# Layer 0 of a two-layer cross-attention kernel: TensorE in four 64x64 tiles, with two PSUM banks for each product

## The chip, the cores and the metric

The kernel runs on one core of a Trainium2 chip. The time is the device time of one execution in microseconds (us): 2881.49 us, the median of three runs (2879.67 to 2883.18).

The core has a matrix engine (TensorE, PE in the profile), which multiplies a stationary operand, loaded beforehand (PEld), with a moving one and writes to PSUM; three engines for the rest (VectorE is DVE, ScalarE is ACT, GpSimd is POOL); and DMA queues, most of them issued by SyncE (SP). Each engine runs its own list of instructions in the written order, and semaphores make one wait for another.

TensorE's array of 128x128 cells can be split into tiles. "128*64" in a profile row means 128 rows (contraction) by 64 columns (outputs) for one tile, so that two such tiles fill the array. Each tile takes its own matmuls.

## The reference

Four batches, two layers of cross-attention, all in 32-bit floats. `x` is 4 x 1024 x 512, the context 4 x 1024 x 384, and there are 16 heads in each layer.

```
layer 0 (heads of 64):
  h = layernorm(x) * gamma + beta
  Q = h Wq;  K = context Wk;  V = context Wv
  A = softmax(Q K^T) / 8
  x = x + (A V) Wo + bo
layer 1 (heads of 32):
  xn = x / rms(x) * norm_w
  q = xn wq;  k, v = split(context wkv)
  q, k = rotate(q), rotate(k), each scaled to length 1
  x = x + (softmax(q k^T * sqrt(32)) v) wout
```

## The kernel before

Everything is one program, written out by Python. For each batch, layer 0 comes first and then layer 1. Layer 0 takes the 16 heads as eight pairs (`p`), as two heads fill 128 partitions. Within a pair there are eight steps (`i`), one for each 128 queries; the class `Attention0` (line 355) writes one step:

- `scores` (line 363): four matmuls of 64 rows by 128 columns, 512 keys each, into two PSUM tiles of two banks, one for each head. The two heads run in two row tiles.
- For each head the negated maximum on DVE (line 393), the exponential on ACT with its sum (394), on DVE the transposition of the step before (402) and the reciprocal (398), on POOL the scaling (399).
- After every second step `regroup` (408) sends the transposed weights to other partitions, in 16 DMAs on SP's queue.
- `product` (421): once two blocks of two steps are queued, the odd step multiplies the older one with V: 8 x 2 matmuls of 128 rows by 64 columns, 256 queries each, into one PSUM bank, which ACT copies out (line 138).
- Then `Units.fill` (71) puts other TensorE work into the rest of the step.

This other work is a queue of small units, each with a cost in us: the projections of the next but one pair (`pair_units`, line 311: K in 6 units, Q in 8, V in 8), the output sums of finished pairs (`add_units`, line 287; a DVE addition for each 128 rows, line 296), and in the last two pairs the first projections of layer 1. Each goes through the helper `matmul` (line 161), which splits the outputs into two column tiles in layer 0 and four in layer 1. The driver (from line 757) counts what is still to be done in the batch, spreads it evenly over the steps that are left, and takes off 3.5 us where a step has a product; `fill` pops units until the sum that is owed is used up. So TensorE's list within a step is: scores, perhaps a product, then units.

PSUM has eight banks here. Four belong to the two score tiles. The other four are handed out in turn by `bank` (line 128), to products, projections, transpositions and sums.

The order on ACT follows the same writing order: both exponentials of a step, the copy of the product, and then the copies of the units of that step.

Layer 1 (`Attention1`, line 556) has 64 steps a batch, with scores in four row tiles (32*128) and everything else in four column tiles (128*32). During its second half, the first projections of the next batch's layer 0 are made.

Of the kernel before, what the change touches and what calls it, by code (L numbers as in the profile page):

```python
# [38 lines left out]
P = 128  # L39
S = 1024  # L40
# [15 lines left out]

class Units:


    def __init__(self):  # L60
        self.todo = deque()
        self.owed = 0.0
        self.done = 0

    def add(self, units):
        self.todo.extend(units)

    def total(self):
        return sum(c for c, _ in self.todo)

    def fill(self, us):
        self.owed += us
        while self.todo and self.owed > 0:
            self.owed -= self.one()
        if not self.todo:
            self.owed = min(self.owed, 0.0)

    def one(self):
        c, f = self.todo.popleft()
        f()  # L80
        self.done += 1
        return c

    def end(self):

        return self.done + len(self.todo)

    def until(self, end):
        while self.done < end:
            self.owed -= self.one()  # L90
# [20 lines left out]
def xattn_kernel(ctx: ExitStack, tc: tile.TileContext, a: dict, out: bass.AP):  # L111
# [14 lines left out]
    which = {"n": 0, "from": 0, "cols": 2, "kept": None}  # L126

    def bank(name):

        while True:  # L130
            which["n"] = which["n"] + 1 if which["n"] < 3 else which["from"]
            if which["n"] != which["kept"]:
                break
            which["kept"] = None
        return ps_f.tile([P, 512], F32, tag=f"f{which['n']}", name=name)
# [31 lines left out]

    def rsqrt(o, v):

        nc.gpsimd.tensor_tensor(o, v, nhalf[:, : v.shape[1]], ALU.pow)  # L170


    def context_units(b, ct):
# [11 lines left out]
        def turn_over(h, k):  # L185
            if k == 0:
                if h == 0:
                    both = sb.tile([P, NC_, S], F32, tag="ctxT", bufs=1, name=f"cT_{b}")
                    ct.extend([both[:, :, :512], both[:, :, 512:]])
            pp = bank(f"ptc_{b}_{h}_{k}")  # L190
            for t in range(4):
                nc.tensor.transpose(pp[:, t * P : (t + 1) * P], raws[4 * h + t][:, k * P : (k + 1) * P], ident)
            evac(ct[h][:, k, :], pp)

# [8 lines left out]
    def norm_units(b, layer, hT, rows):  # L203
# [39 lines left out]
        def turn_over(h, k):  # L243
            if k == 0:
                hT.append(sb.tile([P, NQ, 512], F32, tag="hT", bufs=2, name=f"hT{layer}_{b}_{h}"))
            pp = bank(f"pth{layer}_{b}_{h}_{k}")
            for t in range(4):
                nc.tensor.transpose(pp[:, t * P : (t + 1) * P], got[h][t][:, k * P : (k + 1) * P], ident)
            if layer == 0:
                nc.scalar.activation(  # L250
                    hT[h][:, k, :], pp, AF.Identity, bias=cols[:, 1, k : k + 1], scale=cols[:, 0, k : k + 1]
                )
            else:
                nc.scalar.activation(hT[h][:, k, :], pp, AF.Copy, scale=cols[:, 2, k : k + 1])

# [31 lines left out]
    def add_units(xt, lhs, w, name, cs, then=None):  # L287
# [3 lines left out]
        def one(t, i, pp=[None]):  # L291
            if i == 0:
                pp[0] = bank(f"{name}_{t}")
            matmul(pp[0], lhs(cs[i])[:, t * P : (t + 1) * P], w(cs[i]), i == 0, i == n - 1)
            if i == n - 1:
                nc.vector.tensor_add(xt[t], xt[t], pp[0])  # L296
                if then is not None:
                    then(t)

        return [[(0.86, lambda t=t, i=i: one(t, i)) for i in range(n)] for t in range(NT)]  # L300
# [10 lines left out]
    def pair_units(b, p, w, hT, ct, res):  # L311

        n = f"{b}_{p}"

        def project(what, src, w0, nk, h, k, st={}):
            if what == "kT" and h == 0 and k == 0:
                qk = sb.tile([P, 2, S], F32, tag="qk", bufs=3, name=f"qk0_{n}")
                res["kT"], res["qT"] = qk[:, 0], qk[:, 1]
            if k == 0:
                st["pp"] = bank(f"p{what}0_{n}_{h}")  # L320
            matmul(st["pp"], w()[:, w0 + k, :], src[h][:, k, :], k == 0, k == nk - 1)
            if k < nk - 1:
                return
            if what == "qT":
                evac(res[what][:, h * 512 : (h + 1) * 512], st["pp"])
            else:
                quarters = res[what].rearrange("p (g c i) -> p c g i", g=4, i=32)
                evac(quarters[:, 4 * h : 4 * h + 4], st["pp"].rearrange("p (c g i) -> p c g i", g=4, i=32))

        def values(h, t, st={}):  # L330
            if h == 0 and t == 0:
                res["v"] = sb.tile([P, NT, P], F32, tag="v", bufs=3, name=f"v0_{n}")
            if t == 0:
                st["pp"] = bank(f"pv0_{n}_{h}")
            for k in range(NC_):
                matmul(
                    st["pp"][:, t * P : (t + 1) * P],
# [5 lines left out]
            if t == 3:  # L343
                evac(res["v"][:, 4 * h : 4 * h + 4, :].rearrange("p t f -> p (t f)"), st["pp"])

        return {
# [8 lines left out]
    class Attention0:  # L355
# [7 lines left out]
        def scores(self, p, i, pr):  # L363
            n = f"{self.b}_{p}_{i}"
            sc = [score(f"s0_{n}_{j}") for j in range(2)]
            for kb in range(2):
                for j in range(2):
                    nc.tensor.matmul(  # L368
                        sc[j][:, kb * 512 : (kb + 1) * 512],
                        pr["qT"][r[j], i * P : (i + 1) * P],  # L370
                        pr["kT"][r[j], kb * 512 : (kb + 1) * 512],
                        start=True,
                        stop=True,
                    )
            return sc

        def step(self, p, i, pr, us):
            n = f"{self.b}_{p}_{i}"
            sc = self.scores(p, i, pr)
            m = sb.tile([P, 2], F32, tag="m", bufs=3, name=f"m_{n}")  # L380
# [25 lines left out]
            self.u.fill(us)  # L406
# [14 lines left out]
        def product(self):  # L421
# [4 lines left out]
            av = bank(f"av_{self.b}_{p}_{q}")  # L426
            for k in range(NT):
                for j in range(2):
                    nc.tensor.matmul(  # L429
                        av[r[j], :W].rearrange("p (t a i) -> p t a i", t=BQ, a=4),  # L430
                        pr["v"][:, k, r[j]],
                        eT[:, j, :, :, k * 32 : (k + 1) * 32],
                        start=k == 0,
                        stop=k == NT - 1,
                    )
            evac(pr["vals"][:, q * W : (q + 1) * W], av[:, :W])
# [16 lines left out]
    def rotated_chains(dst, src, nk, w, name, tmp):  # L453
# [10 lines left out]
        def project(t0, i, k):  # L464
            if i == 0 and k == 0:
                tiles[t0] = [bank(f"{name}_p{t0}")]
                if which["from"] == 0:
                    which["kept"] = which["n"]
            pp = tiles[t0][0]
# [3 lines left out]
            if i == TH - 1 and k == nk - 1:  # L473
                rotate(t0, pp)

# [19 lines left out]
        def turn_over(t0):  # L495
            t1 = tiles.pop(t0)
            pt = bank(f"{name}_t{t0}")
# [7 lines left out]
            nc.scalar.copy(dst()[:, :, t0 * P : (t0 + TH) * P], pt.rearrange("p (g t) -> p g t", g=2))  # L505

# [30 lines left out]
    def value_chains(v, wv, ct, name):  # L537
        def one(t0, i, k, st={}):
# [4 lines left out]
            matmul(st["pp"][:, i * FH : (i + 1) * FH], lhsT, wv[:, k, :], k == 0, k == NC_ - 1)  # L543
            if i == TH - 1 and k == NC_ - 1:
                pv = st["pp"].rearrange("p (t g d) -> p g t d", t=TH, g=2)
                for g in range(2):
                    nc.scalar.copy(v[g][:, t0 : t0 + TH, :], pv[:, g])

# [141 lines left out]
    def prepare_units(b):  # L690
# [7 lines left out]
        def project(p):  # L698
# [5 lines left out]
            return begin | pair_units(b, p, lambda: w[p], st["hT"], st["ct"], st["pairs"][p])  # L704
# [5 lines left out]
        def order(other):  # L710

            pairs = [project(p) for p in range(2)]
# [24 lines left out]
            ), pairs[1]["v"]  # L737
# [3 lines left out]
    work = Units()  # L741
    st, order = prepare_units(0)
# [14 lines left out]
    for b in range(B):  # L757
# [7 lines left out]
        for p in range(NPAIR):  # L765
# [10 lines left out]
            elif p % 2 == 0:  # L776
# [6 lines left out]
                    (p - 2, p - 1),  # L783
                )
# [29 lines left out]
            n = 7 * (p == 0)  # L814
# [58 lines left out]
        for half in range(2):  # L873
            n = 0
            if half == 0:
# [11 lines left out]
                base = work.done  # L887
# [41 lines left out]
        which["from"], which["cols"] = 0, 2  # L929
        if b == B - 1:  # L930
            tail = flat(adds[1][6:])
        else:
            outs = add_units(
                xt, lambda n, o=o: o[n], lambda n, w=wo1[1]: w[:, n % 2, :], f"po1_{b}_1", (2, 3), store
# [40 lines left out]
```

## Time and profile before

| what | us |
|---|---|
| median of three runs | 2881.49 |
| span of the profiled execution | 2885.9 |
| PE busy | 2827.9 |
| DVE busy | 2248.4 |
| ACT busy | 1430.1 |
| layer 0 scores (line 368), 2048 records | 519.1 |
| layer 0 products (line 429), 4096 records | 472.8 |
| layer 0 maxima on DVE (line 393), 512 | 602.9 |
| layer 0 transpositions on DVE (line 402), 512 | 619.9 |

The profile is that of one execution; its span, 2885.9 us, is its own time from the first to the last instruction, and it is 0.15% above the median of the runs. A 32-bit matmul shows as two records of weight load and two of matmul. The records' durations overlap, so the sum of a group is more than the time it takes; the distance between the starts of two groups tells what the first one cost. In four stretches, one for each batch, the eight pairs of layer 0 take about 444, 429, 430 and 430 us.

### The profile page before, as it was taken

What the parts mean: (1) busy time and instruction counts of PE and PEld (TensorE: products, weight loads), DVE (VectorE), ACT (ScalarE), POOL (GpSimd) and SP (SyncE); (2) the same over time, 40 slices, a digit from 0 to 9 for tenths busy, and PEclk for the clock granted to TensorE, in tenths of its full rate; (3) what the DMA queues carried; (4) which work ended last, traced back from release to release, by engine and by line L of the source; (5) the groups of instructions that cost most, each with busy time, mean ns of one, the idle gap of its engine ahead of it and who ended that gap; (6) DMA issues with size and microseconds to landing.
All of it is one profiled execution on the core that took longest, in us unless ns stands there. A gap on an engine that the chain in (4) does not pass through costs nothing.

```text
span 2885.9 us, 65749 instructions
## 1 busy us (share of the span) xinstructions
PE 2827.9 (98%) x26888; PEld 1420.5 (49%) x26888; DVE 2248.4 (78%) x3008; ACT 1430.1 (50%) x2276; POOL 947.8 (33%) x776
## 2 busy tenths in 40 slices
PE   8999999999999999999999999999999999999998
PEld 4444445555444445555544445455554444445543
DVE  5677786898777778589877777959987777785987
ACT  4443443666444444466643444446664444444664
POOL 2343344320134335342023433534202333353410
PEclk9999999999999999999999999999999999999999
DMA  5887776010298777501039887740105887773000
GB/s 138 183 188 176 174 170 150 22 37 25 73 207 189 180 173 174 128 22 36 26 93 205 195 184 165 178 103 22 37 26 121 203 196 184 163 173 83 2 2 31
DMA packets 177549, 348.81 MB, mean 121 GB/s; under 512 B 37600, under 2 KB 93152, under 8 KB 177248
## 3 DMA queue, kind: packets, MB, share of 16 engines
q1 hardware_dynamic: 175920, 343.96, 50.9%
q8 instruction: 212, 3.47, 0.5%
q14 instruction: 89, 0.73, 0.1%
q10 hardware_dynamic: 1328, 0.66, 0.1%
HBM read 67.64 MB, written 8.39 MB: 26 GB/s over the span
## 4 chain that ended last, share of the span: by engine, by line
PE 87%; DVE 3%; SPq 3%; DMA 2%; ACT 2%; issue 1%; POOL 1%; ACTq 0%; DVEq 0%
PE s L368 16%; PE av L429 14%; PE po L166 11%; PE s L586 9%; PE av L635 8%; PE pv L166 7%; PE pqT L166 7%; PE pkT L166 5%; PE q_p L166 4%; PE k_p L166 3%; SPq L413 2%; DMA eT<-e 1%; ACT e L596 1%; PE av L659 1%; DVE m L393 1%
## 5 line engine op out<-in xcount | busy, mean ns | idle before, releaser
L393 DVE TENSOR_REDUCE m<-s 128x1 f32<-128x1024 f32 x512 | 602.9, 1219 | 381.5 <-PE s L368 380.9
L596 ACT ACTIVATE e<-s 128x1024 f32<-128x1024 f32 x512 | 496.5, 1022 | 295.3 <-PE s L586 288.9
L399 POOL TENSOR_SCALAR raw<-raw,li 128x1024 f32<-128x1024 f32 x256 | 286.1, 1118 | 734.1 <-DVE li L398 725.6
L368 PE MATMUL s<-qk 64*128 64x512 f32 x2048 | 519.1, 616 | 3.0 <-ACT e L394 2.2
L394 ACT ACTIVATE e<-s,m 128x1024 f32<-128x1024 f32 x256 | 282.8, 1109 | 465.2 <-DVE m L393 224.3
L394 ACT ACTIVATE raw<-s,m 128x1024 f32<-128x1024 f32 x256 | 285.1, 1114 | 458.7 <-DVE m L393 458.7
L429 PE MATMUL av<-eT,v 128*64 128x256 f32 x4096 | 472.8, 384 | 12.2 <-DMA eT<-e 9.1
L399 POOL TENSOR_SCALAR e<-e,li 128x1024 f32<-128x1024 f32 x256 | 286.1, 1118 | 472.6 <-DVE li L398 240.3
L429 PEld LDWEIGHTS av<-eT,v 128*64 128x64 f32 x4096 | 288.2, 137 | 232.1 <-issue 94.8
L605 DVE TENSOR_TENSOR both<-e 128x512 f32<-128x512 f32 x512 | 342.8, 702 | 64.3 <-ACT e L596 62.2
L368 PEld LDWEIGHTS s<-qk 64*128 64x128 f32 x2048 | 184.8, 186 | 285.2 <-issue 168.8
L586 PE MATMUL s<-q,k 32*128 32x256 f32 x4096 | 308.0, 402 | 5.3 <-ACT q L505 2.7
L402 DVE STREAM_TRANSPOSE e<-raw 128x1024 f32<-128x1024 f32 x256 | 309.9, 1228 | 1.7 <-DMA eT<-e 1.7
L402 DVE STREAM_TRANSPOSE e<-e 128x1024 f32<-128x1024 f32 x256 | 310.0, 1229 | 0.2
L586 PEld LDWEIGHTS s<-q,k 32*128 32x128 f32 x4096 | 193.9, 185 | 142.5 <-ACT e L596 66.4
L166 PE MATMUL pqT<-hT,w 128*64 128x512 f32 (+1 forms) x1216 | 241.9, 597 | 2.5 <-ACT hT L250 2.5
L166 PE MATMUL po<-wo,vals 128*64 128x512 f32 x1024 | 234.6, 596 | 0.0
L166 PEld LDWEIGHTS pv<-w,cT 128*64 128x64 f32 (+1 forms) x3360 | 170.4, 132 | 41.8 <-issue 34.1
L296 DVE TENSOR_TENSOR x<-x,po 128x512 f32<-128x512 f32 x200 | 131.7, 678 | 70.4 <-PE po L166 69.7
L166 PE MATMUL pv<-w,cT 128*64 128x128 f32 (+1 forms) x3360 | 184.3, 274 | 0.9 <-ACT hT L250 0.7
L166 PE MATMUL pkT<-cT,w 128*64 128x512 f32 (+1 forms) x912 | 182.0, 597 | 0.0
L607 DVE TENSOR_TENSOR both<-both 128x1024 f32<-128x1024 f32 x128 | 159.7, 1248 | 4.4
(87 smaller groups left out, 2801.3 us busy)
## 6 DMA issues: line engine op xcount, KB each, us to landing
eT<-e SPq DMA_DIRECT2D x2048, 128.0 KB, 2.4
xr<-in_x_dram SPq DMA_DIRECT2D x32, 256.0 KB, 4.0
wo<-in_Wo_dram SPq DMA_DIRECT2D x16, 512.0 KB, 3.9
x<-in_x_dram SPq DMA_DIRECT2D x32, 256.0 KB, 5.0
out_dram<-x SPq DMA_DIRECT2D x32, 256.0 KB, 2.7
w<-in_Wq_dram SPq DMA_DIRECT2D x31, 256.0 KB, 3.3
c<-in_ctx_dram SPq DMA_DIRECT2D x32, 192.0 KB, 3.9
wkv<-in_wkv_dram SPq DMA_DIRECT2D x16, 384.0 KB, 3.3
```

What stands on the lines that cost most here:

```text
L166: nc.tensor.matmul(o[rr], lhsT[:, rr], rhs, start=start, stop=stop)
L368: nc.tensor.matmul(sc[j][:, kb * 512 : (kb + 1) * 512], pr["qT"][r[j], i * P : (i + 1) * P], pr["kT"][r[j], kb * 512 : (kb + 1) * 512], st ...
L393: nc.vector.tensor_reduce(m[:, j : j + 1], sc[j], AX.X, ALU.max, negate=True)
L394: nc.scalar.activation(e[j], sc[j].rearrange("p (g s) -> p g s", g=4), AF.Exp, bias=m[:, j : j + 1], accum_out=l[:, j : j + 1])
L399: nc.gpsimd.tensor_scalar(e[j], e[j], li[:, j : j + 1], HD0**-0.5, ALU.mult, ALU.mult)
L402: self.turn = [lambda j=j: nc.vector.transpose(self.e[:, :, i % BQ * 2 + j, :], e[j]) for j in range(2)]
L429: nc.tensor.matmul(av[r[j], :W].rearrange("p (t a i) -> p t a i", t=BQ, a=4), pr["v"][:, k, r[j]], eT[:, j, :, :, k * 32 : (k + 1) * 32], ...
L586: nc.tensor.matmul(sc[j // 2][:, j % 2, c, :], kT[rr, g, k * P : (k + 1) * P], qT[rr, g, qb * WQ : (qb + 1) * WQ], start=True, stop=True,)
L596: nc.scalar.activation(e, sc[u], AF.Exp, scale=float(np.sqrt(np.float32(HD1))))
L605: nc.vector.tensor_add(into[:, 2 * u : 2 * u + 2, :], es[u][:, :, 0, :], es[u][:, :, 1, :])
L607: nc.vector.tensor_add(acc, acc, into)
L635: nc.tensor.matmul(self.av[rr, 0, :], v[g][:, 2 * kk + c, rr], es[j // 2][:, j % 2, c, :], start=first and c == 0, stop=end and c == 1,)
```

## The change

Everything that layer 0 does on TensorE within its steps is put into tiles of 64 rows by 64 columns, of which four fill the array.

- Scores: each matmul is split into two of 64 queries.
- Products: the contraction over 128 keys is split into two halves, in two row tiles, each of which writes its own bank. ACT copies the first bank and DVE adds the second.
- Projections of layer 0 and output sums: two results are made together, in a pair of banks (0, 1) or (2, 3). In a first turn row tile 0 works for the first result and row tile 1 for the second; in the second turn they change over. Row tiles must not write one bank at once, so between the turns there is a barrier: a copy of one element on ACT (`turned`) waits for the first turn's last matmul, and the second turn's first matmul waits for this copy.
- The planner: such a double result is a `Group` with two turns. The second turn counts as ready when 1.5 us of other TensorE work has passed since the first (`RIPE`). A second group may be begun when the first isn't ready and a pair of banks is free. In even steps (`spare`) no group is begun if what is owed doesn't reach to end the open one, and groups are ended until at most one pair of banks is held, since the next step's product needs the other.
- Banks: the one (or the pair) that has been free the longest is taken, instead of one after the other.

Layer 1 keeps its shapes, and so do the first pair's projections, the last output sum of layer 0 and the transpositions. The diff, cut to its core:

```diff
+class Group:
+    def __init__(self, turns):
+        self.turns = [deque(t) for t in turns]
+        self.since = 0.0
+    def left(self):
+        return sum(c for t in self.turns for c, _ in t)
...
 class Units:
+    RIPE = 1.5
...
-    def fill(self, us):
+    def passed(self, us):
+        for _, g in self.open:
+            g.since += us
+    def fill(self, us, spare=False):
         self.owed += us
-        while self.todo and self.owed > 0:
+        while (self.todo or self.open) and self.owed > 0:
+            if spare and self.open and self.starts_next() and self.owed < self.open[0][1].left():
+                break
             self.owed -= self.one()
+        while spare and self.pairs_held() > 1:
+            self.owed -= self.one()
...
+    def ready(self):
+        return [g for _, g in self.open if g.turns[0] or g.since >= self.RIPE]
+    def starts_next(self):
+        return not self.ready() and self.todo and isinstance(self.todo[0], Group) and self.pairs_held() < 2
+    def pick(self):
+        ready = self.ready()
+        if ready:
+            return ready[0]
+        if self.starts_next():
+            g = self.todo.popleft()
+            self.open.append((self.begun, g))
+            self.begun += 1
+            return g
+        if self.todo and not isinstance(self.todo[0], Group):
+            return None
+        return self.open[0][1]
     def one(self):
-        c, f = self.todo.popleft()
+        g = self.pick()
...
+        turn = next(t for t in g.turns if t)
+        c, f = turn.popleft()
         f()
-        self.done += 1
+        self.passed(c)
+        if not g.turns[0] and turn is g.turns[0]:
+            g.since = 0.0
...
-    which = {"n": 0, "from": 0, "cols": 2, "kept": None}
+    which = {"from": 0, "cols": 2, "clock": 0}
+    freed, held = [0, 1, 2, 3], set()
...
     def bank(name):
-        while True:
-            which["n"] = which["n"] + 1 if which["n"] < 3 else which["from"]
-            if which["n"] != which["kept"]:
-                break
-            which["kept"] = None
-        return ps_f.tile([P, 512], F32, tag=f"f{which['n']}", name=name)
+        n = min((n for n in range(which["from"], 4) if n not in held), key=lambda n: freed[n])
+        return take([n], [name])[0]
+    def two_banks(name):
+        free = [p for p in ((0, 1), (2, 3)) if not held & set(p)]
+        p = min(free, key=lambda p: max(freed[n] for n in p))
+        return take(p, [f"{name}_a", f"{name}_b"])
+    def free(n, later=0):
+        which["clock"] += 1
+        held.discard(n)
+        freed[n] = which["clock"] + later
...
+    sixty = [slice(j * 64, (j + 1) * 64) for j in range(2)]
+    turned = const.tile([1, 1], F32, name="turned")
+    def behind(inst, other):
+        tc.add_manual_dep(inst.ins, other.ins.name, SYNC, reason="row tiles change banks")
+    def quarters(st, os, lhsTs, rhss, turn, start, stop, last):
+        for i in range(2):
+            u = i ^ turn
+            for j in range(2):
+                mm = nc.tensor.matmul(
+                    os[u][sixty[j]], lhsTs[u][sixty[i], sixty[j]], rhss[u][sixty[i]], start=start, stop=stop
+                )
+                if turn == 1 and st["turned"] is not None:
+                    behind(mm, st["turned"])
+                    st["turned"] = None
+        if turn == 0 and last:
+            st["turned"] = nc.scalar.copy(turned, ident[:1, :1])
+            behind(st["turned"], mm)
...
+        def project_both(what, src, w0, nk, k, turn, st):
+            first, last = k == turn == 0, k == nk - 1 and turn == 1
...
+            if first:
+                st["pp"] = two_banks(f"p{what}0_{n}")
+            quarters(
...
+            if last:
+                for h in range(2):
+                    placed(what, h, st["pp"][h])
...
+                "k": group(0.86, NC_, lambda k, turn, st: project_both("kT", ct, NQ, NC_, k, turn, st)),
+                "q": group(0.86, NQ, lambda k, turn, st: project_both("qT", hT, 0, NQ, k, turn, st)),
+                "v": group(0.66, 4, values_both),
...
 def scores(self, p, i, pr):
...
                 for j in range(2):
-                    nc.tensor.matmul(
-                        sc[j][:, kb * 512 : (kb + 1) * 512],
-                        pr["qT"][r[j], i * P : (i + 1) * P],
...
+                    for q in range(2):
+                        q0 = i * P + q * 64
+                        nc.tensor.matmul(
+                            sc[j][sixty[q], kb * 512 : (kb + 1) * 512],
+                            pr["qT"][r[j], q0 : q0 + 64],
...
             sc = self.scores(p, i, pr)
+            self.u.passed(1.71)
...
                 self.product()
-            self.u.fill(us)
+                self.u.passed(3.41)
+            self.u.fill(us, spare=i % BQ == 0)
...
-            av = bank(f"av_{self.b}_{p}_{q}")
+            av = two_banks(f"av_{self.b}_{p}_{q}")
             for k in range(NT):
-                for j in range(2):
...
+                for n, (_, pp) in enumerate(av):
+                    for j in range(2):
+                        nc.tensor.matmul(
+                            pp[r[j], :W].rearrange("p (t a i) -> p t a i", t=BQ, a=4),
+                            pr["v"][sixty[n], k, r[j]],
+                            eT[sixty[n], j, :, :, k * 32 : (k + 1) * 32],
...
-            evac(pr["vals"][:, q * W : (q + 1) * W], av[:, :W])
+            vals = pr["vals"][:, q * W : (q + 1) * W]
+            evac(vals, av[0][1][:, :W])
+            free(av[0][0])
+            nc.vector.tensor_add(vals, vals, av[1][1][:, :W])
+            free(av[1][0])
...
+    work.pairs_held = lambda: sum(bool(held & set(p)) for p in ((0, 1), (2, 3)))
...
-            n = 7 * (p == 0)
+            n = 2 * (p == 0)
```

## The prediction

> **What bounds the kernel now.** I read the page first, then TensorE's own order in time, then all engines over two steps of layer 0, then the busy times of one batch's layer 0.
>
> ```profile
> span 2885.9 us, 65749 instructions
> PE 2827.9 (98%) x26888; PEld 1420.5 (49%) x26888; DVE 2248.4 (78%) x3008; ACT 1430.1 (50%) x2276; POOL 947.8 (33%) x776
> ...
> PE 87%; DVE 3%; SPq 3%; DMA 2%; ACT 2%; issue 1%; POOL 1%; ACTq 0%; DVEq 0%
> ```
>
> TensorE (PE) is the bound: 98% busy, 87% of the chain that ended last. Whether that is useful work is seen in its order in time (start, duration, engine, line, tiles, shape, count):
>
> ```profile
> 203.37 1.99 PE L368 MATMUL s<-qk 64*128 64x512 f32 x8
> 205.28 3.67 PE L429 MATMUL av<-eT,v 128*64 128x256 f32 x32
> 208.79 1.48 PE L166 MATMUL pv<-w,cT 128*64 128x128 f32 x24
> 210.20 1.99 PE L368 MATMUL s<-qk 64*128 64x512 f32 x8
> 212.11 2.84 PE L166 MATMUL pv<-w,cT 128*64 128x128 f32 x48
> 214.78 1.89 PE L166 MATMUL po<-wo,vals 128*64 128x512 f32 x8
> 216.60 1.99 PE L368 MATMUL s<-qk 64*128 64x512 f32 x8
> ```
>
> Two tiles run at once, and two records of 512 columns take 0.428 us (from the distances inside the weight loads of one projection: 901.15, 901.58, 902.01). So scores are worth 4 x 0.428 = 1.71 us, yet the next group starts 205.28 - 203.37 = 1.91 us later: 0.20 us are lost where the tile shape goes from 64*128 to 128*64. The way back costs 216.60 - 214.78 - 1.71 = 0.11 us. Between two groups of one shape it is about 0.05 us (225.76 to 229.24 for 16 records: 3.48 against 3.43). This is all that the change can win in TensorE's work: columns times tiles stay the same.
>
> The second view is one even step (scores at 237.44), the next scores (243.80) and what lies between:
>
> ```profile
> 237.44 1.99 PE L368 MATMUL s<-qk 64*128 64x512 f32 x8
> ...
> 239.36 2.79 PE L166 MATMUL pkT<-cT,w 128*64 128x512 f32 x12
> 239.46 2.36 DVE L393 TENSOR_REDUCE m<-s 128x1 f32<-128x1024 f32 x2 [2.50 <-PE s L368]
> 240.78 1.11 ACT L394 ACTIVATE raw<-s,m 128x1024 f32<-128x1024 f32 x1 [2.63 <-DVE m L393]
> ...
> 241.91 1.11 ACT L394 ACTIVATE raw<-s,m 128x1024 f32<-128x1024 f32 x1
> ...
> 242.92 0.19 ACT L394 ACTIVATION_READ_ACCUMULATOR raw<-s,m 128x1 f32 x1
> ...
> 243.01 0.57 ACT L138 COPY qk<-pkT 128x512 f32<-128x512 f32 x1
> ...
> 243.80 1.99 PE L368 MATMUL s<-qk 64*128 64x512 f32 x8
> ```
>
> Two things are to be seen. First, a chain of 5.6 us runs from scores to the end of the second exponential (237.44 to 243.02), which frees the second score tile; the next scores can't be done before. Today a step has 6.2 to 7.2 us of PE work, so this is hidden. Second, ScalarE (ACT) works in order: the copy of pkT, whose last matmul began before 241.98, runs only at 243.01, after both exponentials. Whatever is issued to ACT among a step's projections is done no earlier than about 5.6 us after that step's scores began.
>
> The busy times of the second batch's layer 0 (columns: window, length, PE, PEld, DVE, ACT, POOL, clock, DMA share, GB/s):
>
> ```profile
> 749.00:1178.00 429.00, 425.83 (x2944) 205.97 (x2940) 334.00 (x438) 184.47 (x338) 168.68 (x147) 1.00 0.77 177
> ```
>
> The clock is full, DVE has 95 us to spare per batch. 64 steps of 6.70 us make the 429.
>
> **The change, part by part.** One batch (the second) is worked out and taken four times.
>
> *Same shape everywhere (gain).* Steps without layer 1's units number 54 of 64; in pairs 6 and 7 ten steps still run layer 1's key and value projections at 128*64 and keep their switches. 54 x (0.20 + 0.11) = 16.7 us go; at 54 x 2 boundaries the 0.05 us of equal shapes stays, 5.4 us. Net -11.3.
>
> *Four tiles instead of two.* The count of matmuls doubles, each with a quarter of the array, so the sum of columns per tile stays. No row shows 64*64. Four row tiles (layer 1 scores, 32*128, 16 records of 256 columns from 698.31 to 699.39) take 1.08 us, of which 0.22 us is the switch: 4 x 0.214, full speed. Four column tiles with 128 columns (pv at 128*32, 48 records in 1.49 us) take 0.11 us a round, full speed too. I take 0; the upper end is in the rivals.
>
> The Trainium skill, "TensorE: Matmul & The Clock Gate", section "Measured speedup vs the span model", speaks against it: four row tiles ran 3.07 times as fast as one, not 4. By that the some 400 us of a batch's matmuls (429 less 64 x 0.31 of switches and a few of waits) would grow by about 30%, an estimate of 480 us in all; the layer 1 row contradicts it, so I don't use it.
>
> *The product's second half.* Per product one DVE add of 128x256 from PSUM, 0.42 us (nearest row: the rotation's 128x256 products at line 482, 415 ns), 32 per batch, 13.4 us on DVE's 334 of 429. It stands behind the step's reciprocals and ahead of the next maximum, which today waits 1.2 to 2.5 us for scores: hidden, 0; the upper end is 128 x 0.42 = 54 us. A group's two copies out of its banks (0.58 us each on ACT) and two adds (0.68 each on DVE) now come together at its end; both engines have that room during the next scores (1.71 us), so 0.
>
> *The barrier between the turns.* Each projection group now runs through its inputs, then waits for a one-element ACT copy before it runs through them again with banks exchanged. The copy itself is 0.2 us (accumulator reads: 0.19), but it stands in ACT's queue behind both exponentials. Behind the waiting matmul stands everything on PE, in order, the next scores among it. If the second turn comes in a later step, the copy is long done. If it comes in the same step, it can start only 5.6 + 0.2 + about 0.15 = 5.95 us after scores began, while the planner thinks 1.5 us of other work enough.
>
> *The planner's order.* This decides, so I followed its rules with its own costs: at p = 0 it owes 292 us over 64 steps, 4.57 an even step and 4.57 - 3.5 = 1.07 an odd one (which carries the product). Groups cost 2 x 2.58 (k), 2 x 3.44 (q), 2 x 2.64 (v), 2 x 1.72 (output sums). An even step that has a finished first turn and too little owed to end that group now stops and leaves the rest to the odd step. Example: step 0 of pair 4 runs three value units (1.98), has 2.23 left against 2.64 needed, and stops; the odd step then has 6.9 us.
>
> Counted so, eleven even steps stop early, with these fills (pair.step): 0.0 2.64, 0.4 1.72, 1.2 3.44, 1.4 3.44, 2.0 3.04, 3.2 2.58, 3.6 1.72, 4.0 1.98, 4.4 2.58, 4.6 3.44, 5.0 3.50; together 30.1. Such a step is scores 1.75 plus its fill, but the 5.6 us chain is no longer covered: 11 x (5.6 - 1.75) - 30.1 = 12.3 us lost. The long odd step gives nothing back, as PE work is the bound there. Four odd steps hold only a product (5.2 us): 1.5 us. Together +13.8.
>
> Ten second turns start in the step of their first turn, after this much fill: 0.3 3.44, 0.6 2.64, 1.0 3.44, 2.2 2.58, 3.0 2.38, 3.4 2.58, 4.2 2.58, 6.4 2.62, 6.6 2.61, 7.2 1.72; together 26.6. With 0.1 us of boundaries each waits 5.95 - 1.85 - fill: 41 - 26.6 = +14.4.
>
> *Two pairs of banks in place of four single banks.* A group opened in an odd step behind the product takes the product's pair, which is free once DVE has added: reciprocals end 6.76 us after scores (237.44 to 244.07 and 0.12), plus 0.42 and a latency, 7.3 us. In pair 2, step 3, the group starts at about 6.3. Seven such starts would cost 6.7 us; between 0 and that I take half, +3.4, as which pair comes first depends on layer 1's last order.
>
> *What stays.* DMAs and their queues (SP, POOL) are untouched. Layer 1's banks are chosen by age rather than in turn; its waits on bank readers are 10 to 15 us in all, so between -10 and +10; taken as 0.
>
> Sum per batch: -11.3 + 13.8 + 14.4 + 3.4 = +20.3, four times +81. The profiled execution spans 2885.9 us, 4.4 above the median of the runs, 2881.5; the difference is set on the median: 2963.
>
> **The rivals.** (A) *Faster.* The three waits don't come: the planner's stops fall elsewhere or ACT reaches the barrier copies early. Then 4 x -11.3 = -45 remains: 2836. It decides from the point where a batch loses under 11.3 us to waits, a third of what I count. For it: PE at 98% today, so the switches are real. Against: the ACT order above. (B) *Weights of four tiles can't be loaded in 0.107 us* (values, 128 columns). Loads of row tiles take 186 ns against 137 (L368 and L429); a round of 0.186 us adds 48 x 0.079 = 3.8 us a group, 28 groups: +106, 3069. Against: the 128*32 row. (C) *DVE becomes the bound*: the adds come in pairs of 0.68 us now and the 54 us lie on the path: 3017. Against: 1.2 to 2.5 us of idle time before the maxima. (D) *Nothing*: 64*64 still drains between scores and products (no row shows that it doesn't), and the waits are hidden: 2881.
>
> **How the numbers follow.** Forecast 0.61, A 0.20, D 0.05, B 0.06, C 0.08. The time is the forecast's, 2963; its own range, with waits at half or all of what I count and d at both ends, is 2900 to 2990. The range of 8 in 10 reaches from 2850 (leaving out most of A) to 3017 (C in, B out). Less than 0.2% (5.8 us) either way can't be told from no change: faster 0.20, same 0.05, slower 0.75.
>
> **What would show it.** In TensorE's order: scores to products 1.75 us apart in place of 1.91; even steps of 5.6 us next to odd steps of 8 to 9; maxima and exponentials unchanged. In the waits: scores waiting for ACT's exponentials (some 50 us in all) and projections waiting for the one-element copies (some 55 us). PE's busy share falls below 96%. I am wrong if copies run before the step's exponentials, if steps stay at 6 to 7 us, or if a round of four tiles takes more than 0.428 us per 512 columns.

## The result, and the profile after

The changed kernel takes 2952.1 us (median of four runs, 2949.8 to 2954.7) against 2880.6 us for the kernel before, measured beside it: 1.0242 times as long, interval [1.0227, 1.0257]. That is 71.6 us more, where the forecast was 81 more. The profiled execution spans 2947.9 us, 62.0 more than the one of before.

First the page. Its first two lines are the span and the engines' busy times; the third is the chain of work that ended last.

```profile
span 2947.9 us, 89063 instructions
...
PE 2817.8 (96%) x38080; PEld 1551.2 (53%) x38080; DVE 2295.2 (78%) x3136; ACT 1443.0 (49%) x2414; POOL 947.3 (32%) x776
...
PE 9%; ACT 1%; DVE 1%; issue 1%; SPq 0%; POOL 0%; DMA 0%; ACTq 0%
```

TensorE's busy time fell by 10 us while the span grew by 62: the engine is busy for less time and waits more (its share is 95.6%). The chain can't be read here: its shares add up to some 12%, so it breaks off early.

Two steps of the second batch show the two waits. The first is an even step that the planner ended early (pair 3, step 2; start, duration, engine, line, operation):

```profile
941.02 1.90 PE L565 MATMUL s<-qk 64*64 64x512 f32 x16
...
942.73 0.60 PE L259 MATMUL po_b<-wo,vals 64*64 64x512 f32 x2
...
944.27 1.12 ACT L592 ACTIVATE raw<-s,m 128x1024 f32<-128x1024 f32 x1 [3.49 <-DVE m L591]
...
945.40 1.11 ACT L592 ACTIVATE raw<-s,m 128x1024 f32<-128x1024 f32 x1
945.52 3.06 PE L565 MATMUL s<-qk 64*64 64x512 f32 x16
...
948.33 0.65 PE L629 MATMUL av_a<-eT,v 64*64 64x256 f32 x4
```

The output sums follow 942.73 - 941.02 = 1.71 us after the scores, where 1.91 us went from scores to a group of another shape before: equal shapes do what they should. But the next scores start after 4.50 us, when the first exponential has freed the first score tile, and they take 3.06 us instead of 1.90: their other half waits for the second exponential, which ends at 946.51. From 941.02 to the product at 948.33 there are 7.31 us for 1.72 + 2.58 + 1.72 = 6.02 us of matmuls: 1.29 us are lost. The forecast's arithmetic for this step was 5.6 - 1.75 - 2.58 = 1.27.

The second is a second turn in the step in which its first ended (pair 3, step 0):

```profile
926.61 0.59 PE L565 MATMUL s<-qk 64*64 64x512 f32 x2
...
930.64 0.60 PE L259 MATMUL po_b<-wo,vals 64*64 64x512 f32 x2
...
930.99 1.11 ACT L592 ACTIVATE raw<-s,m 128x1024 f32<-128x1024 f32 x1
...
932.09 0.40 ACT L266 COPY turned<-ident 1x1 f32<-1x1 f32 x2
932.32 0.33 PE L259 MATMUL pv_b<-w,cT 64*64 64x128 f32 x2 [1.08 <-ACT turned L266]
```

The one-element copies run right behind the second exponential, 5.48 us after the scores, and the second turn starts 5.71 us after them; the forecast had 5.95. TensorE stands still in between with everything behind it.

Over the whole run the waits answer that were named (engine, line, waited for: us, times, longest):

```profile
PEld s L565 <- ACT raw L592: 54.9, 62, 2.6
...
PEld po_b L259 <- ACT turned L266: 45.9, 25, 3.3
...
PEld pv_b L259 <- ACT turned L266: 11.5, 9, 2.0
PEld pkT_b L259 <- ACT turned L266: 7.7, 5, 1.7
```

Weight loads wait 54.9 us for exponentials and 65.1 us for the copies. A weight load is issued ahead of its matmul, so this is more than what TensorE loses: the matmuls themselves wait 14.2 us for exponentials and 34.5 us for the copies. And one row has grown that the forecast did not mention, the product behind the regroup transfers; first before, then after (by line and shape: busy us, mean ns, idle us before and what ended it):

```profile
L429 PE MATMUL av<-eT,v 128*64 128x256 f32 x4096 | 472.8, 384 | 12.2 <-DMA eT<-e 9.1 <-issue 1.6 <-DMA out_dram<-x 1.1
```

```profile
L629 PE MATMUL av_b<-eT,v 64*64 64x256 f32 x4096 | 470.1, 380 | 17.0 <-DMA eT<-e 13.2 <-DMA x<-in_x_dram 1.7 <-DMA wo<-in_Wo_dram 1.0
```

The second batch's layer 0, answering to the stretch of 429.00 us with TensorE busy for 425.83 (same columns):

```profile
759.00:1205.00 446.00, 424.78 (x5684) 237.26 (x5680) 344.84 (x469) 188.06 (x375) 169.12 (x148) 0.99 0.74 171
```

VectorE has 101 us to spare, so it doesn't explain the 17 us. The clock explains a part: its granted share is 0.99 here and was 1.00 before. In three windows of 3.4 us it is 0.50, each within half a microsecond of the end of a wait of TensorE of 2.1 to 2.5 us. One of them (same columns):

```profile
1165.70:1169.10 3.40, 3.36 (x16) 1.05 (x20) 1.00 (x2) 0.00 (x0) 2.14 (x2) 0.50 0.36 77
```

From 1165.74 on, the rounds of the output sums start some 0.86 us apart there, in place of 0.43. So a window can cost up to 1.7 us, the three some 5 of the 17. Not every long wait has one behind it (the 2.39 us ahead of 1896.52 have none), and what decides that isn't shown. Over the whole execution the granted clock is 0.991, before 0.996; 0.009 of 2947.9 less 0.004 of 2885.9 is some 15 us, an estimate of what this adds to the price of the waits in this execution. The forecast had no such term.

By place: from the first scores of layer 0 to the last, the four batches took 437, 422, 422 and 423 us before and 442, 439, 437 and 434 after, 47 more together. The passages to layer 1, layer 1 and the rest took 288.5 to 290.7 us a batch before and 292.5 to 293.9 after, 14 more together. All of this lies ahead of layer 1's first scores: they start 42.35 us after layer 0's last ones in each batch before, and 44.63 to 46.25 us after them now (46.2 where a window of half clock falls there).

### The profile page after: what moved, and what is told of

Its sections match the earlier page's. It is cut to its first block, busy times and chain, and to the rows that moved or that the text cites. A ratio compares the mean times of both kernels' runs of the same rounds, so it can differ in the third digit from the quotient of the medians.

```text
span 2947.9 us, 89063 instructions
## 1 busy us (share of the span) xinstructions
PE 2817.8 (96%) x38080; PEld 1551.2 (53%) x38080; DVE 2295.2 (78%) x3136; ACT 1443.0 (49%) x2414; POOL 947.3 (32%) x776
## 5 line engine op out<-in xcount | busy, mean ns | idle before, releaser
L565 PE MATMUL s<-qk 64*64 64x512 f32 x4096 | 580.0, 596 | 16.0 <-ACT raw L592 14.2
L592 ACT ACTIVATE raw<-s,m 128x1024 f32<-128x1024 f32 x256 | 285.1, 1114 | 424.0 <-DVE m L591 420.2
L629 PE MATMUL av_b<-eT,v 64*64 64x256 f32 x4096 | 470.1, 380 | 17.0 <-DMA eT<-e 13.2
L629 PE MATMUL av_a<-eT,v 64*64 64x256 f32 x4096 | 475.1, 381 | 2.7 <-ACT k L708 2.7
L565 PEld LDWEIGHTS s<-qk 64*64 64x64 f32 x4096 | 193.0, 134 | 268.1 <-issue 187.3
L629 PEld LDWEIGHTS av_b<-eT,v 64*64 64x64 f32 x4096 | 295.9, 134 | 70.9 <-issue 27.6
L629 PEld LDWEIGHTS av_a<-eT,v 64*64 64x64 f32 x4096 | 274.3, 134 | 100.2 <-issue 35.0
L259 PE MATMUL po_b<-wo,vals 64*64 64x512 f32 x768 | 185.4, 602 | 24.2 <-ACT turned L266 24.0
L259 PE MATMUL po_a<-wo,vals 64*64 64x512 f32 x768 | 183.3, 602 | 4.5 <-ACT v L215 4.5
L259 PE MATMUL pqT_b<-hT,w 64*64 64x512 f32 x800 | 185.1, 590 | 0.0
L259 PE MATMUL pqT_a<-hT,w 64*64 64x512 f32 x800 | 184.9, 589 | 0.0
```

Of the source, the lines that this page charges most:

```text
L259: mm = nc.tensor.matmul(os[u][sixty[j]], lhsTs[u][sixty[i], sixty[j]], rhss[u][sixty[i]], start=start, stop=stop)
L565: nc.tensor.matmul(sc[j][sixty[q], kb * 512 : (kb + 1) * 512], pr["qT"][r[j], q0 : q0 + 64], pr["kT"][r[j], kb * 512 : (kb + 1) * 512], st ...
L592: nc.scalar.activation(e[j], sc[j].rearrange("p (g s) -> p g s", g=4), AF.Exp, bias=m[:, j : j + 1], accum_out=l[:, j : j + 1])
L629: nc.tensor.matmul(pp[r[j], :W].rearrange("p (t a i) -> p t a i", t=BQ, a=4), pr["v"][sixty[n], k, r[j]], eT[sixty[n], j, :, :, k * 32 : ( ...
```

## The experiments

Each ratio is to the kernel before, run on the same chip. The twelve runs came in three groups.

**Taking the barrier and the stops apart.** *Without the exchange:* both turns use the banks in the same order, so nothing must wait; the units' order stays the change's.

```
-            u = i ^ turn
+            u = i
...
-        if turn == 0 and last:
-            st["turned"] = nc.scalar.copy(turned, ident[:1, :1])
-            behind(st["turned"], mm)
+        st["turned"] = None
```

> The second turn keeps the banks of the first, so that no barrier copy is needed; half of the contraction of the projections and output sums is thereby put on the wrong result. Columns, banks, order of units and copies out stay as in the changed kernel. Theory (waits at the barrier, ten of them in a batch, are about 14 us of each batch's loss): 4 x 14 = 56 us go, 2896 us. Rival 1 (64x64 matmuls are slower by themselves, the barrier is hidden): no change, 2952. Rival 2 (DVE's extra additions are the bound): no change, 2952.

Measured: 2917.7 us, ratio 1.0114 [1.0093, 1.0135]. The barrier is worth 1.0242 - 1.0114 = 0.0128, 37 us, not the 56 that were expected. In its place the product's idle time rose from 17.0 to 26.8 us:

```profile
L627 PE MATMUL av_b<-eT,v 64*64 64x256 f32 x4096 | 472.6, 381 | 26.8 <-DMA eT<-e 18.8 <-DVE m L589 2.4 <-DMA x<-in_x_dram 2.1
```

*And with no stops:* the same, and a second turn may follow its first at once, so that units run in the order in which they were added.

```
-    RIPE = 1.5
+    RIPE = 0.0
```

> As the run without exchange (half of the contraction on the wrong result), and a second turn counts as ready at once (RIPE 0), so that a group runs through without a stop in even steps and no second one is begun beside it. Theory: the stops (16 us a batch) and most waits for banks (4 us) go as well: 4 x (14 + 20) = 134 us below the changed kernel, about 2818, which is 2.2% below the kernel before: the worth of the equal shapes alone. Rival 1 (64x64 is slower by itself): stays above 2881. Rival 2 (DVE is the bound): the additions remain, stays above 2881.

Measured: 2881.7 us, ratio 0.9991 [0.9982, 1.0000]: the same as before, where 2818 was expected. Yet the steps are what equal shapes promised. Undisturbed ones take 6.01, 6.03 and 6.89 us, where they took 6.36, 6.38 and 7.24. What was gained there is lost in a few other steps: pair 1, step 3 takes 13.8 us in the second batch. The product's row and SyncE's queue at that place show why (start, duration, queue, line, transfer, count):

```profile
L627 PE MATMUL av_b<-eT,v 64*64 64x256 f32 x4096 | 475.9, 382 | 35.7 <-DMA eT<-e 26.9 <-issue 4.5 <-DMA x<-in_x_dram 3.1
```

```profile
805.69 0.44 SPq L888 DMA_DIRECT2D wo<-in_Wo_dram  x1
806.18 0.51 SPq L383 DMA_DIRECT2D x<-in_x_dram  x1
806.80 14.42 SPq L610 DMA_DIRECT2D eT<-e  x16
821.32 0.53 SPq L1077 DMA_DIRECT2D out_dram<-x  x1
821.89 0.45 SPq L383 DMA_DIRECT2D x<-in_x_dram  x1
822.45 10.90 SPq L610 DMA_DIRECT2D eT<-e  x16
```

SyncE issues 16 regroup transfers for every two steps, one by one; undisturbed an issue takes 0.63 us (10.1 us for 16), and here 10.9 and 14.4. Two steps of 6.02 us last 12.0. With the loads and stores between them the queue has no room, and products wait for their operand. Behind that wait the clock is halved here too: its granted share is 0.50 from 821.8 to 828.6, about half of that step.

*The barrier kept, no stops:* only the line `RIPE = 0.0` in the changed kernel.

> The changed kernel with RIPE 0: groups run through without stops, but each with its barrier, so that 26 second turns in a batch start in the step of their first one, in place of ten. Theory: 54 us of barrier waits a batch in place of 15, 15 us of stops gone: +18 a batch, 3023 us. Rival (the stops are what costs, and the barrier is cheap): 4 x 16 = 64 us faster than the changed kernel, 2888.

Measured: 3075.1 us, ratio 1.0657 [1.0634, 1.0679], 52 above the expectation. Every group now has the barrier within its step, and it costs 1.0657 - 0.9991 = 0.0666, 192 us. Part of this is the clock, whose granted share falls to 0.979 (0.993 in the run above). So the planner's stops are not the dear part: they save far more at the barrier than they cost.

**Part of the change alone.** Scores and products in 64x64 tiles, everything else in two tiles as before (`square` false for projections and output sums).

```
-        def project(p, square=True):
+        def project(p, square=False):
...
-            pairs = [project(p, square=b == 0 and p == 1) for p in range(2)]
+            pairs = [project(p, square=False) for p in range(2)]
...
-                    square=True,
+                    square=False,
```

> Scores and products in 64x64, projections and output sums as before in two column tiles without groups. Theory: no barriers and no stops, but the shape changes now lie between scores or products and projections, as many as before: 2870 to 2895 us, the same as before within 0.5%. Rival 1 (64x64 matmuls are slower by themselves): most of the 71 us of the changed kernel stays, since scores and products are 60% of its 64x64 work: 2920 or more. Rival 2 (DVE's additions on the path): 32 x 0.42 us a batch stay, 2930.

Measured: 2907.0 us, ratio 1.0067 [1.0042, 1.0093], above the range of the theory and below those of the rivals. No gain: steps shrink only from 6.36 to 6.32 us, since each still changes shape once to the projections and back, and the passages grow by some 3 us a batch here too (292.3 against 288.5 to 290.7), 11 of the 20 us by which the profiled execution is longer.

*Banks by age.* The kernel before with the change's choice of banks alone.

```
-        while True:
-            which["n"] = which["n"] + 1 if which["n"] < 3 else which["from"]
...
+        n = min((n for n in range(which["from"], 4) if n not in held), key=lambda n: freed[n])
+        held.add(n)
```

> The kernel before, in which only the choice of banks is that of the change: the one longest free in place of the next in turn (no 64x64 tiles, no pairs of banks, no barrier). Theory (the 14 us lost outside layer 0's steps and the waits of pair 7 come from the choice of banks): 2890 to 2900. Rival (they come from products with a pair of banks, or from the order of units): 2881, as before.

Measured: 2883.8 us, ratio 1.0004 [0.9992, 1.0015]; its passages take 287.6 to 289.2 us. The theory fell: the choice by age costs nothing. As the run above has the longer passages with no 64x64 projections, what is left for them is the product with its pair of banks, two of which are done in each passage. No run has it alone, but the traces agree. Layer 1's first scores come 42.35 us after layer 0's last ones here, as before, and at least 44.62 in the run above. At the first of the two products, VectorE's next work for layer 1 (`xn`) now stands in its queue behind the product's addition, and the transpositions that need it start about 0.9 us later. The second product now waits 0.68 us for ACT to copy out of a bank of its pair (2.7 us in its row over the four batches).

**Moving transfers off SyncE's queue.** The same edit went into four kernels (and into the last version of the next group): 4 of the 16 regroup transfers of two steps are issued by GpSimd.

```
             for g in range(4):
+                eng = nc.gpsimd if g == 3 else nc.sync
                 for k in range(4):
-                    nc.sync.dma_start(eT[32 * g : 32 * (g + 1), k], self.e[32 * k : 32 * (k + 1), g])
+                    eng.dma_start(eT[32 * g : 32 * (g + 1), k], self.e[32 * k : 32 * (k + 1), g])
```

In the kernel without exchange and stops:

> The kernel of the second experiment (both turns straight on, nothing exchanged, so half of each projection's contraction goes to the wrong bank and the result is not the reference's), with 4 of the 16 regroup transfers of two steps issued on POOL's queue in place of SP's. Theory (products wait for regroup transfers because SP issues them one after the other, 16 x 0.63 = 10.1 us per two steps of 12.0): SP's share falls to 12 x 0.63 = 7.6 us, the last transfer lands some 2.5 us earlier, most of the 47 us that products wait go, 2845 to 2860 in place of 2882. Rival 1 (the transfers themselves are the limit, DMA engines 0.8 busy): the waits stay, 2875 to 2885. Rival 2 (POOL is too late to issue them, behind its scaling of the exponentials): slower than 2882.

Measured: 2835.4 us, ratio 0.9832 [0.9813, 0.9852]. The 46 us are there, more than expected. Most of them show in the product's row, whose idle time fell from 35.7 us:

```profile
L628 PE MATMUL av_b<-eT,v 64*64 64x256 f32 x4096 | 466.8, 377 | 5.2 <-DMA eT<-e 5.1
```

The bytes are the same, and the DMA engines' mean busy share in the second batch's layer 0 is 0.74 (0.78 with SyncE alone), so the engines were not the main limit, though in the disturbed step above they were busy for 0.92 of the time (821.8 to 828.6). The Trainium skill says on its page "DMA: Bandwidth & Descriptors", section "Issuing engines are not separate DMA queues", that issuing from several engines saves only the time to issue, "which is usually small relative to the DMA itself". One issue is small here too, 0.63 us where a transfer lands 2.6 us after its issue (median); but sixteen in a row on one queue, 10.1 us of every 12.0, were the limit.

In the changed kernel:

> The changed kernel with nothing but 4 of the 16 regroup transfers of two steps moved from SP's queue to POOL's. Theory (of the 71 us that the change costs, the 20 us by which products wait longer for regroup transfers are a term of their own): 2925 to 2938 in place of 2952. Rival (a product that waits only uses time that the next barrier or the next exponentials would have taken anyway): 2945 to 2955.

Measured: 2927.0 us, ratio 1.0141 [1.0123, 1.0160], as expected; the row of the product's second bank has no idle time left.

In the kernel before:

> The kernel before with the same 4 of 16 transfers on POOL's queue. Theory (before, products wait 2.3 us for transfers in all, as its steps are long enough): 2875 to 2882, hardly a change. Rival (the second queue helps whatever the tiles, so that the 46 us of the experiment without exchange say nothing of the tiles): 2840 to 2860.

Measured: 2874.8 us, ratio 0.9957 [0.9941, 0.9973], 12 us. This is the fastest version with the whole computation. The 2.3 us in the expectation were too few; the product's row before says 12.2 us of idle time, and with two queues 0.4 are left.

In the kernel with stops but no exchange:

> The first experiment's kernel (units in the change's order, with its stops, but no exchange of banks and no barrier, so half of each projection's contraction goes to the wrong bank and the result is not the reference's) with 4 of 16 transfers on POOL's queue. Theory: of its 33 us of waits for transfers most go, 2885 to 2895. Then the stops and the order alone cost 50 to 60 us against the straight order on two queues (2835), and the barrier alone the rest up to the change on two queues, some 40. Rival (short even steps cost nothing by themselves, only by bringing transfers late): 2840 to 2860.

Measured: 2878.5 us, ratio 0.9972 [0.9962, 0.9982]. It is 40 us above the straight order, less than the 50 to 60 expected: the stops cost by themselves, and the rival falls.

**Trying for a better version.** *A second turn a step later:* the units between no longer count as cover.

```
             c, f = self.todo.popleft()
             self.begun += 1
             f()
-            self.passed(c)
             return c
...
         c, f = turn.popleft()
         f()
-        self.passed(c)
```

> The changed kernel, but other units no longer count towards the ripeness of a second turn, only scores and products do: a second turn starts a step later than its first turn ended wherever something else can be done. Theory (the barrier costs where it stands in the step of its first turn): of the waits of 24 to 46 us most go, but more even steps end early, together some 41 us by counting the order of units: about 2911. Rival (the barrier's cost is the hop itself, wherever it stands): 2945 to 2955.

Measured: 2944.6 us, ratio 1.0212 [1.0196, 1.0227]. This is far above the theory and just below the rival's range, though the reason need not be the rival's: weight loads of output sums and values still wait 31.8 and 12.6 us for the copies. By the planner's rules a group whose first turn is over has nothing to wait behind when no other group can begin. The edit removed too few of the waits to tell.

*The same, with output sums in two tiles:* `square` false in the two calls that make them.

> As the run before it in this job, and the output sums of layer 0 and layer 1 stay in two 128x64 tiles with one bank each, as they were before the change, so that they can be put between the first and the second turn of a projection. Theory: few waits are left between turns and short even steps are rarer; counting the order of units gives 26 us a batch less than the change, 2850, but faster steps make products wait for transfers, up to 47 us as in the second experiment: 2850 to 2895, I take 2875. Rival (the exchange costs something everywhere): 2920 or more.

Measured: 2936.1 us, ratio 1.0178 [1.0160, 1.0197]. The theory fell. Here the waits at the barrier are nearly gone, and the time hardly moves:

```profile
PEld s L563 <- ACT raw L590: 29.4, 38, 2.5
PE av_b L627 <- DMA eT<-e: 16.0, 10, 3.4
...
PEld pv_b L257 <- ACT turned L264: 2.0, 3, 0.7
PEld pkT_b L257 <- ACT turned L264: 1.6, 4, 0.4
```

In the third batch, most steps with output sums take 0.3 to 0.8 us more than their columns need, and pair 1, step 3, where transfers come late in the other runs too, loses some 4.7. So shape changes and transfers took back part of it; the arithmetic had 26 us a batch, and the rest of that miss stays open. The number is the rival's here too, and as no run has this kernel without the exchange, the rival is not excluded.

*No exchange at all, and the whole computation:* each half of a projection goes once through its inputs, upper rows into one bank and lower rows into the other, and VectorE adds them; output sums in two tiles, transfers on two queues.

```
+        def summed(to, banks, view):
+            evac(to, view(banks[0][1]))
+            free(banks[0][0])
+            nc.vector.tensor_add(to, to, view(banks[1][1]))
+            free(banks[1][0])
...
+            quarters(st, [pp for _, pp in st["pp"]], [lhsT] * 2, [rhs] * 2, 0, k == 0, k == nk - 1, False)
+            if k == nk - 1:
+                placed_both(what, h, st["pp"])
```

> A version without exchange that computes the whole: each half of a projection goes straight through its inputs, the upper rows' tiles into one bank and the lower rows' into the other, and VectorE adds the second bank as it does for the product; output sums as before the change; 4 of 16 transfers on POOL's queue. No barrier and no stops for one; 48 more additions of 0.68 us a batch on VectorE, 33 us, and a pair of banks is free only when they are done. Theory (barrier, stops and transfers were what ate the gain): 2835 for the straight order and some 28 for the output sums' changes of shape, and up to 15 a batch for banks: 2850 to 2920, I take 2875. Rival (additions or banks decide): over 2930.

Measured: 2895.2 us, ratio 1.0031 [1.0018, 1.0043], within the theory's range. Better than the change by 2%, but not than before: from first to last scores it takes 420.2 us in batches two to four, the kernel before on two queues 419.7. The passages take 292.4 to 293.9 us against 288.9 to 290.1, which is most of the 19 us between the two profiled executions. VectorE's busy time grew to 2384.9 us (83%). What the projections won within the steps has gone elsewhere; changes of shape at the output sums and waits for banks are the likely takers, but no run parts them.

## Why the prediction was right, and where its terms were off

The runs make a table of two columns, with SyncE alone and with GpSimd's help (ratios to the kernel before as it was; a difference of 0.001 is 2.9 us, and two ratios differ by some 0.002 to 0.003 by chance):

| kernel | SyncE alone | two queues |
|---|---|---|
| before | 1 | 0.9957 |
| 64x64, straight order, no exchange | 0.9991 | 0.9832 |
| with the change's order and stops | 1.0114 | 0.9972 |
| with the exchange: the change | 1.0242 | 1.0141 |

The two rows without exchange don't compute the reference's result.

Read downwards, these are the forecast's terms, times four (what the half clock behind waits takes is within each figure):

| step of the prediction | forecast, us | SyncE alone | two queues |
|---|---|---|---|
| same shape everywhere | -45 | -3 | -36 |
| even steps that stop early | +55 | +35 | +40 |
| second turn in the step of its first | +58 | +37 | +49 |
| sum (forecast with +13 for bank pairs) | +81 | +70 | +53 |

*Same shape everywhere.* The mechanism was right and the gain inside the steps larger than taken. The prediction left 0.05 us at each boundary of equal shapes; a step with projections became 0.35 us shorter, against 0.31 for the two switches, so hardly anything is left there. On two queues the stretch from first to last scores fell from 419.7 to 404.4-406.7 us in batches two to four, 13 to 15 us against the 11.3 forecast. Two things were not in the sum. The passages take 2.4 us a batch more on two queues (292.3 against 289.9); the products there wait for banks and delay VectorE, and the added sum, put at nothing, has a part in it. And with SyncE alone the gain is gone, because "DMAs and their queues are untouched" was used as a reason for no cost: the transfers were the same, but the steps that had to cover their issue became shorter.

*Even steps that stop early.* Right. Ten of the eleven steps named are the ones that came in the second batch (all but 0.0). From scores to scores they take 4.5 to 5.4 us rather than 5.6, as the next scores begin on the first free tile and wait for the second one within. Batches two to four pay 10 to 15 us each on two queues (417.1 to 419.8 against 404.4 to 406.7), against 13.8 forecast.

*Second turns in the step of their first.* Right in mechanism and moment (5.71 us after the scores). On two queues each of the ten steps named is longer with the exchange than without in the second batch (by 0.55 to 3.02 us). The term is 12 to 14 us a batch in batches two to four (430.1 to 431.4 against 417.1 to 419.8) for 14.4 forecast.

*Taken four times.* Here both terms were too large: the first batch has another order of units, and pays 3.4 us for stops and 7.2 for the barrier. Pair 1's keys and queries are in 64x64 tiles in that batch alone, and only the later batches hold layer 1's last output sums, which the change puts into 64x64 tiles too.

*Bank pairs.* Put at 13 us over the run. Within the steps, the row of the output sums' first bank shows 4.5 us of waits for a copy out of a bank, and choosing by age costs nothing. The larger price came where the forecast had none, in the passages: 14 us, some 5 of them from half clock (three windows there, of 1.6 us each).

*Four tiles, DVE add, rivals.* Four 64x64 tiles run at the full rate: 16 score records of 512 columns in 1.72 us, the time of 8 before. The Trainium skill's factor of 3.07 is for four row tiles ("TensorE: Matmul & The Clock Gate", "Measured speedup vs the span model"); no such loss shows in the 64x64 tiles here. Weight loads of these tiles take 134 ns and rounds of four value matmuls of 128 columns start 0.11 us apart, so (B) falls. The added sums take 0.40 us each and DVE stays at 78%, so (C) falls, though in the passages they are not hidden. (D) falls with the shorter steps. (A) is what would have come without exchange and with a second queue, 2835 us measured and 2836 forecast; that agreement is partly luck, as its gain in the steps was larger than taken and the passages' cost was missing.

So the sum came out within 10 us because misses cancelled, and that is luck: too much for waits by 41 us and by 13 for bank pairs, too little, by 42, for what transfers, passages and the clock take back. The waits, their places and their sign were not luck.

## What to carry to other kernels

A change that shortens a step must be priced against everything that the step covered: not only the engines' chain but the time in which a queue issues its transfers, which does not shorten with it. A one-element instruction used as a barrier costs what stands ahead of it in its engine's order, here two exponentials, not its own 0.2 us. When two costs of opposite sign meet in a sum, build the version with one of them alone; only that showed that the gain was real and spent elsewhere.

## What was not expected of the hardware

Between groups of equal tile shape TensorE loses next to nothing, while going from 64*128 to 128*64 and back cost 0.31 us a step. One issue on SyncE's queue takes 0.63 us, and 16 of them take 10.1 of the 12.0 us of two steps, which leaves little room for other loads; moving a quarter to GpSimd raised GpSimd's busy time from 947.8 to 1196.9 us in the kernel before, 0.49 us for each of 512 issues, without a delay that shows in the time. Behind some waits (1.3 us and longer) the granted clock was 0.50 for 3.4 us, and the matmuls ran at half rate; a passage with such a window took 1.6 us more to layer 1's first scores (46.25 against 44.63). So a wait can cost more than its length. A direct order between matmuls of two row tiles, with no other engine between them, was not tried, nor were fewer and larger regroup transfers.
